# Ten blocks' own half block as a dense round outside the lists, in a two-layer graph attention kernel

## The chip, the cores and the metric

The kernel runs on one core of one Trainium2 chip. The metric is the device time of a run in microseconds (us), lower is better. The profile is of one execution; its span runs from the first to the last instruction.

## The reference

`x` has 3327 nodes of 512 features, `adj` is 3327 x 3327, sparse, with entries between 0.05 and 1 and a full diagonal. Edges crowd at low node numbers: the chance of an edge falls with the index of both nodes.

```
h = relu(layernorm(x))
x = x + (adj @ (relu(adj @ (h @ W1) + b1) @ W2) + b2)          # layer 0
h = relu(layernorm(x))
type_sum = adj @ h
attn_a = sigmoid(concat[type_sum, h] @ Wa.T + ba)              # attn_b alike
hs = h @ W_sa
scores = (hs @ a_left)[:, None] + (hs @ a_right)[None, :]
e = where(adj != 0, exp(-leaky_relu(scores, 0.01)), 0)
x_a = (e / (sum(e, 1) + 1e-5)) @ hs
x_b = adj @ (h @ W_gcnb) + b_gcnb
x = x + sigmoid(attn_a * x_a + attn_b * x_b)                   # layer 1
```

In layer 1, for each node, two weighted sums over its neighbours' rows of h are needed: one with the weights adj, one with the weights e. Multiplying the sums by the matrices W_gcnb and W_sa afterwards gives x_b and x_a.

## The kernel before, in words

The nodes are padded to 3328 and cut into NB = 26 blocks of 128. The host passes adj transposed, so a row of `adjT` is a source node j and a column a target node i.

*Layer 0* goes twice over all of adjT, in seven chunks of 512 columns (tiles of 128 x 512, or several tiles to a load). In the first pass the matmuls at L512 accumulate `acc_u`; at L516 DVE takes for each tile the largest magnitude in every group of GW = 32 columns (`most`). When a chunk is through, `make_lists` (L382) turns `most` into lists: for each block i and each of its two groups of columns q, in each half of 64 columns h, the numbers of the rows j that have a nonzero entry there. It is a generator that runs a step at a time beside the next chunk: flags, a scan, small matmuls `p_list` (L457), comparisons with `place_col`, sums. The number of a half's places is 64 times the block's number of *rounds*, `rooms[i]`, set by `list_rooms` for the given graph: 9, 8, 7, 6, 6 for blocks 1 to 5, five for 6 to 10, four for 11 to 18, three for the rest, 114 in all. If a list ran over, `overflow` would be set, and a dense branch at the end would do layer 1 anew. Block 0 is dense and is treated by itself ("hub").

For each round and group q, `gather_adj` issues one indirect load on POOL (L139, in `gather`) of 128 pieces of 32 columns of adjT into the tile `ae`. A gather is held behind a matmul of the passes by `pace`. The second pass (`acc_g`, L685) makes layer 0's output, its layernorm and the rows h of layer 1, stores the rows (520 wide, with the right score in column 512) in `h_dram`, and takes for each block the two logits of its own row (`own_logits`, two DVE products, L570).

*Layer 1* is a loop over i = 24 down to 2 (from L945), in which several blocks are in work at a time; the order of the work is written out by hand with `queued`, which puts instructions behind others in issue order. An iteration holds: `attend(i)`, which for each round and q issues an indirect load of 128 rows of h on POOL (L139, tiles `hr` and `rows`, 16 pairs of buffers), adds the scores on DVE (L800), takes the maximum (L804), the masked exponential (L206, ACT L207, L208) and the sum over the sources (L809); `weigh` of the block before the last, p_b (L883) and p_a (L890) on PE; `turn` of the last block, transposes `ptt` (L843) and copies to `tyT` on DVE (L858); the sums of exponentials on PE (L866); `sums(i)`, the neighbour sums `acc` (L829), eight matmuls of 64 x 64 by 512 columns to a round; `finish` of the block weighed (L739 to L764: DVE and ACT, a load of x1 on the SP queue and a store of the output on it); `copy_out` (ACT, L902 and L906). The first gather of attend(i) is paced behind the sums of an earlier block (LEAD = 3, or 4 for the blocks with high numbers). A block with more than SEG = 4 rounds does attend and sums in segments. After the loop block 1 and what is still open are finished.

Of the kernel before, what the change touches and what calls it, by code (L numbers as in the profile page):

```python
# [9 lines left out]
F32 = mybir.dt.float32  # L10
# [8 lines left out]
P = 128  # L19
# [15 lines left out]
LEAST_LOGIT = -88.0  # L35


def list_rooms(n_blocks):

    rooms = [0, 9, 8, 7, 6, 6] + 5 * [5] + 8 * [4]
    return (rooms + n_blocks * [3])[:n_blocks]


# [1 line left out]
def kernel(  # L47
# [23 lines left out]
    NCH = len(chunks)  # L71
    NG = NP // GW
    rooms = list_rooms(NB)
    first = [2 * sum(rooms[:i]) for i in range(NB)]
    NL = 2 * sum(rooms)

# [39 lines left out]
    overflow = kept([P, 1], "overflow", I32)  # L116


    ae = [kept([P, 2 * r, 2 * GW], f"ae{i}") if r else None for i, r in enumerate(rooms)]

    def segments(i):
        n = -(-rooms[i] // SEG)
        cuts = [-(-rooms[i] * k // n) for k in range(n + 1)]
        return list(zip(cuts, cuts[1:]))
    hubp = ctx.enter_context(tc.tile_pool(name="hubp", bufs=6))
    a_hub = hubp.tile([P, NB, P], F32, tag="a_hub", name="a_hub", bufs=1)
# [21 lines left out]
    def gather_adj():  # L148

        for i in range(1, NB):  # L150
            r = rooms[i]
            for k0, k1 in segments(i):
                for q in range(2):
                    for k in range(k0, k1):
                        while (i, q) not in listed:
                            yield None
                        f = first[i] + q * r + k
                        yield gather(
                            ae[i][:, 2 * k0 + q * (k1 - k0) + k - k0, :GW], adj_groups,
                            row_a[:, f : f + 1], NP * NG - 1,  # L160
                        )

    columns = gather_adj()

# [51 lines left out]
    with (  # L216
# [95 lines left out]
        MG = CW // GW  # L312
        NT = NB + 1
        begin = kept0([P, MG, NB], "begin", BF16)
        before = kept0([P, P], "before", BF16)
        shift = kept0([P, P], "shift", BF16)
        every = kept0([P, P], "every", BF16)
        steps = [kept0([P, MG, NT], f"step{k}", BF16) for k in range(2)]
        limit = kept0([P, NG], "limit", F32)
        size = kept0([P, NG], "size", F32)  # L320
        lower = kept0([P, 1], "lower", F32)
        place_row = kept0([P, max(rooms) * HALF], "place_row", F16)
        place_col = kept0([P, NL], "place_col", F32)
        group_col = kept0([P, NL], "group_col", F16)

        def make_constants():

            nc.vector.memset(begin, 1.0)
            nc.vector.memset(begin[:, :, 0:1], 0.0)
            for t in steps:  # L330
                nc.vector.memset(t[:, :, NB:NT], 1.0)
                nc.vector.memset(t[0:1, :, NB:NT], 0.0)
            yield
            nc.vector.memset(every, 1.0)

            for t, op, base in ((before, ALU.is_gt, 0), (shift, ALU.is_equal, -1)):
                nc.vector.memset(t, 1.0)
                nc.gpsimd.affine_select(
                    t, t, pattern=[[1, P]], compare_op=op, fill=0.0, base=base,
                    channel_multiplier=-1,  # L340
                )
            yield

            nc.vector.memset(lower, 1.0)
            nc.gpsimd.affine_select(
                lower, lower, pattern=[[0, 1]], compare_op=ALU.is_ge, fill=0.0, base=-HALF,
                channel_multiplier=1,
            )
            first_iota = nc.gpsimd.iota(
                place_row, pattern=[[1, max(rooms) * HALF]], base=0, channel_multiplier=0,  # L350
                allow_small_or_imprecise_dtypes=True,
            )
            tc.add_manual_dep(
                first_iota.ins, scaled[6].ins.name,
                mybir.DependencyInfo(mybir.DependencyClass.Sync, mybir.DependencyReason.DATA),
                reason="not among the first tiles",
            )
            behind = queued(first_iota)
            nc.gpsimd.memset(limit[:, :NQ], float(2 * NP))
            for r in sorted(set(rooms[1:])):  # L360
                i0, n = rooms.index(r), rooms.count(r)
                cols = slice(first[i0], first[i0] + n * 2 * r)
                nc.gpsimd.memset(limit[:, NQ * i0 : NQ * (i0 + n)], float(r * HALF))
                nc.gpsimd.iota(
                    place_col[:, cols], pattern=[[0, 2 * n], [HALF, r]], base=0,
                    channel_multiplier=1, allow_small_or_imprecise_dtypes=True,
                )
                nc.gpsimd.iota(
                    group_col[:, cols], pattern=[[NQ, n], [1, 2], [0, r]], base=NQ * i0,
                    channel_multiplier=0, allow_small_or_imprecise_dtypes=True,  # L370
                )
            yield
            for t, by in ((place_col, -float(HALF)), (group_col, 2.0)):
                nc.vector.scalar_tensor_tensor(
                    t, lower.to_broadcast([P, NL]), by, t, op0=ALU.mult, op1=ALU.add
                )
            yield
            for t in ae[1:]:
                nc.gpsimd.memset(t[:, :, :GW], 0.0)
            behind.close()  # L380

        def make_lists(c, most):  # L382
# [7 lines left out]

            flag = small([P, MG, NB], "flag", BF16)
            nc.vector.tensor_scalar(flag[:, :n, :], most[:, :n, :], 0.0, None, op0=ALU.is_gt)

            upto = small([P, MG, NB], "upto", BF16)
            flat = "p b j -> p (b j)"
# [97 lines left out]
        for c in range(NCH):  # L493
# [37 lines left out]
            with tc.issue_after(chunk_end.ins):  # L531
                if c == 1:
                    load_weights()
                if 0 < c <= HUB_LOADS:
                    load_hub(c - 1)
            lists = make_lists(c, most)
            next(lists)

# [25 lines left out]
                junk, h, 1.0, w_rows[:, s, :], op0=ALU.mult, op1=ALU.mult, accum_out=into  # L564
            )

        def own_logits(i, junk):

            for s in range(2):
                nc.vector.scalar_tensor_tensor(  # L570
                    junk, hrow[i % NR][:, :D], 1.0, w_own[:, s, :], op0=ALU.mult, op1=ALU.mult,
                    accum_out=node[i][:, 1 + s : 2 + s],
                )
            nc.vector.tensor_tensor(node[i][:, 1:3], node[i][:, 1:3], bab_row, ALU.add)
# [4 lines left out]
        def make_h1(c, sT):  # L579
# [49 lines left out]
            for i in blocks:  # L629
                store_next()  # L630

                if c < NCH - 2:
                    own_logits(i, l0w.tile([P, D], BF16, tag="junk", name=f"junk_{i}", bufs=1))
                yield

        rows_made = set()
# [130 lines left out]
    with tc.tile_pool(name="spw", bufs=2) as spw:  # L767
# [8 lines left out]
        def attend(i, seg):  # L776
# [10 lines left out]
            e = both[:, :, GW:]  # L787
            hr = taken[i][k0] = []
            for k in range(n):
                hr.append(next(pairs))  # L790
                for q in range(2):
                    f = first[i] + q * r + k0 + k
                    with queued(gathered[0]):
                        gathered[0] = gather(
                            hr[k][:, q, :], h_dram[:, :], row_h[:, f : f + 1], NP - 1
                        )
                    lead = LEAD[i < NB - 8]
                    if k0 + k + q == 0 and len(combined) >= lead:
                        pace(gathered[0], combined[-lead])
                nc.vector.tensor_tensor(  # L800
                    e.rearrange("p (q k) i -> p k q i", q=2)[:, k],
                    s_l, hr[k][:, :, D : D + 1].to_broadcast([P, 2, GW]), ALU.add,
                )
# [7 lines left out]
            )  # L811
            if k0:
                last = nc.vector.tensor_tensor(es, es, part, ALU.add)
            return last, exp

        def sums(i, seg):

            k0, k1 = seg  # L820
            n = k1 - k0
            if k0 == 0:
                taken[i]["acc"] = [bank(psA, f"acc_{i}_{h}") for h in range(2)]
            both = ae[i][:, 2 * k0 : 2 * k1, :]
            for k in range(n):
                for q in range(2):
                    for h in range(2):
                        half_p = slice(h * HALF, (h + 1) * HALF)
                        added = nc.tensor.matmul(  # L829
                            taken[i]["acc"][h][q * HALF : (q + 1) * HALF, :],  # L830
                            both[half_p, q * n + k, :], taken[i][k0][k][half_p, q, :D],
                            start=(k0 + k == 0), stop=(k1 == rooms[i] and k == n - 1),
                        )
            return added

# [83 lines left out]
        def some_logits(k, inst):  # L919
            n = len(late_rows)  # L920
            with queued(inst):
                for i in late_rows[n * k // 3 : n * (k + 1) // 3]:
                    own_logits(i, a_hub[:, :KD, :].rearrange("p k i -> p (k i)"))

        some_logits(0, made[0])
        for seg in segments(NB - 1):
# [190 lines left out]
```

## Time and profile before

| What | Value |
|---|---|
| Median of three runs | 836.6 us (833.45, 836.6, 841.8) |
| Profiled execution: span | 840.2 us (its time is told as this span) |
| Granted TensorE clock, mean of the span | 0.973 |
| Matrix engine (PE) matmul busy | 781.6 us, 3615 instructions |
| DVE busy | 515.6 us, 1658 instructions |
| ACT busy | 187.6 us, 396 instructions |
| POOL busy | 493.4 us, 513 instructions |
| Gathers from adjT / of rows of h | 228 / 140 + 88 |
| DMA traffic | 200.14 MB |
| Layer 1's loop, i = 24 to 2 | 471.2 to 798.3 us |

In a row of groups, "L829 PE MATMUL acc<-hr,ae" means line 829, the engine, the operation, the tile that is written and those that are read; then the count, the busy time, the mean duration in ns, and the time for which the engine stood still just before, with what ended most of it. "issue" there is waiting for nothing that the profile shows. In a table of stretches the columns are the stretch, its length, the busy times (and counts) of PE, of PE's weight loads, of DVE, ACT and POOL, the granted clock, the DMA share and GB/s.

### The profile page before, as it was taken

What the parts mean: (1) busy time and instruction counts of PE and PEld (TensorE: products, weight loads), DVE (VectorE), ACT (ScalarE), POOL (GpSimd) and SP (SyncE); (2) the same over time, 40 slices, a digit from 0 to 9 for tenths busy, and PEclk for the clock granted to TensorE, in tenths of its full rate; (3) what the DMA queues carried; (4) which work ended last, traced back from release to release, by engine and by line L of the source; (5) the groups of instructions that cost most, each with busy time, mean ns of one, the idle gap of its engine ahead of it and who ended that gap; (6) DMA issues with size and microseconds to landing.
All of it is one profiled execution on the core that took longest, in us unless ns stands there. A gap on an engine that the chain in (4) does not pass through costs nothing.

```text
span 840.2 us, 12143 instructions
## 1 busy us (share of the span) xinstructions
PE 781.6 (93%) x3615; PEld 416.9 (50%) x3615; DVE 515.6 (61%) x1658; ACT 187.6 (22%) x396; POOL 493.4 (59%) x513
## 2 busy tenths in 40 slices
PE   9999899999799999999999599799998999999795
PEld 7774344445443444444464366455554555454363
DVE  7778989999646866685775455345535353443342
ACT  7770000000002313033052022122222222121121
POOL 3202756676677777776716555666766767667400
PEclk9999999999799999999999799899999999999798
DMA  8787998898578989998958556787788867777600
GB/s 272 242 292 227 330 283 262 285 299 276 151 236 297 368 281 306 319 343 284 345 180 260 158 182 196 216 227 217 225 225 215 228 203 227 207 210 209 187 26 30
DMA packets 106891, 200.14 MB, mean 238 GB/s; under 512 B 16801, under 2 KB 30656, under 8 KB 106816
## 3 DMA queue, kind: packets, MB, share of 16 engines
q1 hardware_dynamic: 72592, 124.40, 45.2%
q0 software_dynamic: 25536, 63.74, 27.9%
q10 hardware_dynamic: 8688, 11.15, 3.8%
q8 instruction: 30, 0.49, 0.2%
q14 instruction: 45, 0.37, 0.1%
HBM read 179.39 MB, written 20.55 MB: 238 GB/s over the span
## 4 chain that ended last, share of the span: by engine, by line
PE 66%; issue 18%; DMA 7%; DVE 5%; another core or an unknown queue 3%; ACT 1%; SPq 0%; ACTq 0%; DVEq 0%
PE acc L829 14%; PE p_b L883 12%; PE p_a L890 11%; PE acc_g L685 10%; PE acc_u L512 5%; PE acc_hub L644 3%; DMA a<-in_adjT_dram 3%; PE ptt L843 3%; PE pu L291 3%; PE px L587 2%; DMA W_sa_sb<-in_W_sa_dram 1%; PE pt L283 1%; DMA xb<-in_x_dram 1%; DVE junk L563 1%
## 5 line engine op out<-in xcount | busy, mean ns | idle before, releaser
L139 POOL DMA_INDIRECT ae<-in_adjT_dram,row_a x228 | 246.4, 1081 | 151.6 <-issue 57.8
L139 POOL DMA_INDIRECT hr<-h_rows,row_h x140 | 144.1, 1029 | 64.5 <-issue 30.8
L685 PE MATMUL acc_g<-a,g 128*128 128x512 f32 (+1 forms) x364 | 160.3, 575 | 5.7 <-DMA a<-in_adjT_dram 3.8
L512 PE MATMUL acc_u<-a,rows 128*128 128x512 f32 (+1 forms) x364 | 159.9, 578 | 2.8 <-DMA a<-in_adjT_dram 2.2
L139 POOL DMA_INDIRECT rows<-h_rows,row_h x88 | 90.7, 1031 | 69.2 <-DVE e_hub L206 20.3
L883 PE MATMUL p_b<-W_g_sb,tyT 128*128 128x257 f32 x416 | 102.0, 395 | 16.3 <-issue 15.7
L516 DVE TENSOR_REDUCE most<-a 128x16 f32<-128x512 f32 (+1 forms) x182 | 110.6, 638 | 6.1 <-DMA a<-in_adjT_dram 5.2
L685 PEld LDWEIGHTS acc_g<-a,g 128*128 128x128 f32 x364 | 67.0, 192 | 85.5 <-issue 61.1
L883 PEld LDWEIGHTS p_b<-W_g_sb,tyT 128*128 128x128 f32 x416 | 78.3, 193 | 48.5 <-issue 19.3
L890 PE MATMUL p_a<-W_sa_sb,tyT 128*128 128x512 f32 (+2 forms) x216 | 97.5, 590 | 3.5 <-issue 3.1
L512 PEld LDWEIGHTS acc_u<-a,rows 128*128 128x128 f32 x364 | 66.5, 194 | 58.7 <-issue 51.9
L829 PE MATMUL acc<-hr,ae 64*64 64x512 f32 x560 | 81.7, 612 | 3.2 <-issue 2.3
L858 DVE COPY tyT<-ptt 128x512 f32<-128x512 f32 x51 | 34.9, 686 | 54.2 <-PE acc L829 21.8
L890 PEld LDWEIGHTS p_a<-W_sa_sb,tyT 128*128 128x128 f32 x216 | 41.1, 193 | 47.1 <-issue 45.6
L208 DVE SCALAR_TENSOR_TENSOR ae<-ae 128x192 f32<-128x192 f32 (+2 forms) x36 | 12.5, 368 | 79.1 <-issue 29.9
L829 PE MATMUL acc<-rows,ae 64*64 64x512 f32 x352 | 49.0, 607 | 1.7 <-issue 1.4
L829 PEld LDWEIGHTS acc<-hr,ae 64*64 64x64 f32 x560 | 30.9, 137 | 39.2 <-issue 37.9
L748 ACT ACTIVATE f<-f 128x2 f32<-128x2 f32 x26 | 5.3, 203 | 166.9 <-DVE f L747 118.4
L300 ACT ACTIVATE gT<-acc_u,b_col 128x512 f32<-128x512 f32 (+1 forms) x7 | 4.6, 657 | 157.1 <-issue 101.3
L563 DVE SCALAR_TENSOR_TENSOR junk<-rows,w_rows 128x512 bf16<-128x512 f32 x52 | 35.7, 686 | 3.0 <-issue 0.5
L716 DVE TENSOR_TENSOR xb<-xb,b_row 128x512 f32<-128x512 f32 x26 | 17.7, 689 | 30.4 <-DMA xb<-in_x_dram 19.6
L843 PEld LDWEIGHTS ptt<-ident,ty 128*128 128x128 f32 x208 | 24.5, 144 | 19.1 <-issue 18.2
(142 smaller groups left out, 907.5 us busy)
## 6 DMA issues: line engine op xcount, KB each, us to landing
a<-in_adjT_dram SPq DMA_DIRECT2D x338, 256.0 KB
h_rows<-rows SPq DMA_DIRECT2D x26, 260.0 KB
x<-in_x_dram SPq DMA_DIRECT2D x26, 256.0 KB
xb<-in_x_dram SPq DMA_DIRECT2D x26, 256.0 KB
x<-xb ACTq DMA_DIRECT2D x26, 256.0 KB
x1b<-x SPq DMA_DIRECT2D x26, 256.0 KB
out_dram<-va SPq DMA_DIRECT2D x25, 256.0 KB
ae<-in_adjT_dram,row_a POOLq DMA_INDIRECT x228
```

Source lines behind the costliest of these rows:

```text
L139: return nc.gpsimd.indirect_dma_start(out=dst, out_offset=None, in_=table, in_offset=bass.IndirectOffsetOnAxis(ap=rows, axis=0), bounds_ch ...
L291: nc.tensor.matmul(pu[:, :HID], hT[:, k, :], W1_sb[:, k, :], start=(k == 0), stop=(k == KD - 1))
L512: added = nc.tensor.matmul(acc[:, :w], u[j], a[:, :w], start=(j == 0), stop=(j == NB - 1))
L516: nc.vector.tensor_reduce(most[:, : w // GW, j], a[:, :w].rearrange("p (b i) -> p b i", i=GW), axis=AX.X, op=ALU.max, apply_absolute_value ...
L563: return nc.vector.scalar_tensor_tensor(junk, h, 1.0, w_rows[:, s, :], op0=ALU.mult, op1=ALU.mult, accum_out=into)
L644: nc.tensor.matmul(acc_hub[k], s, hrow[i % NR][:, :D], start=(i == 0), stop=(i == NB - 1))
L685: added = nc.tensor.matmul(acc[:, :w], g[j], a[:, j % per, :], start=(j == 0), stop=(j == NB - 1))
L829: added = nc.tensor.matmul(taken[i]["acc"][h][q * HALF : (q + 1) * HALF, :], both[half_p, q * n + k, :], taken[i][k0][k][half_p, q, :D], s ...
L843: moved = nc.tensor.transpose(pt[:, k * P : (k + 1) * P], ty[h][:, k * P : (k + 1) * P], ident)
L858: last = nc.vector.tensor_copy(dst, src)
L883: nc.tensor.matmul(p_b[n][:, :WH], tyT[:, k, 0, :], W_g_sb[:, k, n * WH : (n + 1) * WH], start=(k == 0), stop=(k == KD - 1),)
L890: last = nc.tensor.matmul(p_a[:, c0:c1], tyT[:, k, 1, :], W_sa_sb[:, k, c0:c1], start=(k == 0), stop=(k == KD - 1),)
```

## The change

For the ten blocks in `OWN` (1, 6, 7, 8, 12, 13, 14, 15, 17, 18) the sources in a target's own half block of 64 nodes leave the lists. They make one round of their own, round 0, with row j of half h in the place j: it needs no list, since its rows are consecutive.

- The entries of adjT for that round come by `load_own`: two plain loads on ACT's queue for each block (64 rows x 2 x 32 columns each), at the ends of chunks in the first pass.
- The rows of h for it come by one plain load on SP's queue into `h_own` (128 rows, three buffers), which serves both groups q, instead of two gathers.
- In `make_lists` the flags of the chunk's OWN blocks are multiplied by `apart`, which is 0 where a row lies in the group's own half block.
- `own_logits` of these ten blocks moves from the second pass into `attend`, where it reads `h_own`.
- `list_rooms` becomes 8, 7, 6, 5, 5 for blocks 1 to 5, four for 6 to 11, three for the rest: 97 list rounds, and with the ten dense ones 107 rounds. There are 194 gathers of each kind.
- `place_col` and `limit` are kept in 16-bit floats, `size` in bfloat16.

```diff
+OWN = 1, 6, 7, 8, 12, 13, 14, 15, 17, 18
-    rooms = [0, 9, 8, 7, 6, 6] + 5 * [5] + 8 * [4]
+    rooms = [0, 8, 7, 6, 5, 5] + 6 * [4]
     return (rooms + n_blocks * [3])[:n_blocks]
...
+    extra = [int(i in OWN) for i in range(NB)]
...
-                    for k in range(k0, k1):
+                    for k in range(max(k0, extra[i]), k1):
...
+    def load_own(i):
+
+        n = segments(i)[0][1]
+        for h in range(2):
+            rows = slice(i * P + h * HALF, i * P + (h + 1) * HALF)
+            nc.scalar.dma_start(
+                ae[i][h * HALF : (h + 1) * HALF, 0 : n + 1 : n, :GW],
+                adjT[rows, rows].rearrange("j (q i) -> j q i", i=GW),
+            )
...
+            own = [i - c0 // P for i in range(c0 // P, (c0 + w) // P) if extra[i]]
+            if own:
+                b0, b1 = own[0], own[-1] + 1
+                own = flag[:, b0 * NQ : b1 * NQ, c0 // P + b0 : c0 // P + b1]
+                nc.vector.tensor_tensor(
+                    own, own, apart[:, b0 * NQ : b1 * NQ, b0:b1], ALU.mult
+                )
...
                     load_hub(c - 1)
+                    for i in OWN:
+                        if c0 <= i * P + CW < c0 + CW:
+                            load_own(i)
...
-                if c < NCH - 2:
-                    own_logits(i, l0w.tile([P, D], BF16, tag="junk", name=f"junk_{i}", bufs=1))
+                if c < NCH - 2 and not extra[i]:
+                    own_logits(
+                        i, hrow[i % NR],
+                        l0w.tile([P, D], BF16, tag="junk", name=f"junk_{i}", bufs=1),
+                    )
...
-                hr.append(next(pairs))
-                for q in range(2):
-                    f = first[i] + q * r + k0 + k
+                if k0 + k < extra[i]:
+                    h = spw.tile([P, ROW], F32, tag="h_own", name=f"h_own_{i}", bufs=3)
+                    nc.sync.dma_start(h, h_dram[i * P : (i + 1) * P, :])
+                    hr.append(h.unsqueeze(1).to_broadcast([P, 2, ROW]))
+                    lists = ()
+                else:
+                    hr.append(next(pairs))
+                    lists = range(2)
+                for q in lists:
+                    f = first[i] + q * r + k0 + k - extra[i]
...
-                    if k0 + k + q == 0 and len(combined) >= lead:
+                    if k0 + k + q == extra[i] and len(combined) >= lead:
                         pace(gathered[0], combined[-lead])
...
             if k0:
                 last = nc.vector.tensor_tensor(es, es, part, ALU.add)
+            elif extra[i]:
+                own_logits(i, hr[0][:, 0, :], spw.tile([P, D], BF16, tag="junk", name=f"junk_{i}"))
```

In the built program the first three loads of `h_own` (18, 17, 15) stand on SP's queue ahead of the loop's first store of the output; each later one stands ahead of a store that is one iteration or more before its use (14 before the store of 20, 13 before that of 19, 12 of 17, 8 of 16, 7 of 15, 6 of 14, 1 of 10).

More of the change, by code (lines that the diff above doesn't have):

```diff
@@ L116 @@
     overflow = kept([P, 1], "overflow", I32)
-    ae = [kept([P, 2 * r, 2 * GW], f"ae{i}") if r else None for i, r in enumerate(rooms)]
+    ae = [
+        kept([P, 2 * (r + extra[i]), 2 * GW], f"ae{i}") if r else None for i, r in enumerate(rooms)
+    ]
     def segments(i):
-        n = -(-rooms[i] // SEG)
-        cuts = [-(-rooms[i] * k // n) for k in range(n + 1)]
+        r = rooms[i] + extra[i]
+        n = -(-r // SEG)
+        cuts = [-(-r * k // n) for k in range(n + 1)]
         return list(zip(cuts, cuts[1:]))
@@ L153, in gather_adj @@
                 for q in range(2):
-                    for k in range(k0, k1):
+                    for k in range(max(k0, extra[i]), k1):
                         while (i, q) not in listed:
                             yield None
-                        f = first[i] + q * r + k
+                        f = first[i] + q * r + k - extra[i]
                         yield gather(
@@ L314 @@
         begin = kept0([P, MG, NB], "begin", BF16)
+        apart = kept0([P, MG, CW // P], "apart", BF16)
         before = kept0([P, P], "before", BF16)
@@ L318 @@
         steps = [kept0([P, MG, NT], f"step{k}", BF16) for k in range(2)]
-        limit = kept0([P, NG], "limit", F32)
-        size = kept0([P, NG], "size", F32)
+        limit = kept0([P, NG], "limit", F16)
+        size = kept0([P, NG], "size", BF16)
         lower = kept0([P, 1], "lower", F32)
         place_row = kept0([P, max(rooms) * HALF], "place_row", F16)
-        place_col = kept0([P, NL], "place_col", F32)
+        place_col = kept0([P, NL], "place_col", F16)
         group_col = kept0([P, NL], "group_col", F16)
@@ L329, in make_constants @@
             nc.vector.memset(begin[:, :, 0:1], 0.0)
+            nc.vector.memset(apart, 1.0)
+            for b in range(CW // P):
+                for h in range(2):
+                    groups = slice(NQ * b + 2 * h, NQ * b + 2 * h + 2)
+                    nc.vector.memset(
+                        apart[h * HALF : (h + 1) * HALF, groups, b : b + 1], 0.0
+                    )
             for t in steps:
@@ L565, in score, with own_logits @@
             )
-        def own_logits(i, junk):
+        def own_logits(i, h, junk):
             for s in range(2):
                 nc.vector.scalar_tensor_tensor(
-                    junk, hrow[i % NR][:, :D], 1.0, w_own[:, s, :], op0=ALU.mult, op1=ALU.mult,
+                    junk, h[:, :D], 1.0, w_own[:, s, :], op0=ALU.mult, op1=ALU.mult,
                     accum_out=node[i][:, 1 + s : 2 + s],
@@ L630, in make_h1 @@
                 store_next()
-                if c < NCH - 2:
-                    own_logits(i, l0w.tile([P, D], BF16, tag="junk", name=f"junk_{i}", bufs=1))
+                if c < NCH - 2 and not extra[i]:
+                    own_logits(
+                        i, hrow[i % NR],
+                        l0w.tile([P, D], BF16, tag="junk", name=f"junk_{i}", bufs=1),
+                    )
                 yield
@@ L831, in sums @@
                             both[half_p, q * n + k, :], taken[i][k0][k][half_p, q, :D],
-                            start=(k0 + k == 0), stop=(k1 == rooms[i] and k == n - 1),
+                            start=(k0 + k == 0), stop=(k1 == rooms[i] + extra[i] and k == n - 1),
                         )
@@ L922, in some_logits @@
                 for i in late_rows[n * k // 3 : n * (k + 1) // 3]:
-                    own_logits(i, a_hub[:, :KD, :].rearrange("p k i -> p (k i)"))
+                    own_logits(i, hrow[i % NR], a_hub[:, :KD, :].rearrange("p k i -> p (k i)"))
         some_logits(0, made[0])
```

## The prediction

> **What bounds the kernel now.** I read the page's busy shares first, then the slices, the chain, the rows of the gathers, and last the busy times by stage.
>
> ```profile
> span 840.2 us, 12143 instructions
> PE 781.6 (93%) x3615; PEld 416.9 (50%) x3615; DVE 515.6 (61%) x1658; ACT 187.6 (22%) x396; POOL 493.4 (59%) x513
> ...
> PE   9999899999799999999999599799998999999795
> POOL 3202756676677777776716555666766767667400
> ...
> PE 66%; issue 18%; DMA 7%; DVE 5%; another core or an unknown queue 3%; ACT 1%; SPq 0%; ACTq 0%; DVEq 0%
> ...
> L139 POOL DMA_INDIRECT ae<-in_adjT_dram,row_a x228 | 246.4, 1081 | 151.6 <-issue 57.8
> L139 POOL DMA_INDIRECT hr<-h_rows,row_h x140 | 144.1, 1029 | 64.5 <-issue 30.8
> ...
> L139 POOL DMA_INDIRECT rows<-h_rows,row_h x88 | 90.7, 1031 | 69.2 <-DVE e_hub L206 20.3
> ```
>
> PE carries the chain, but 18% of it is "issue": PE stood still with no wait that the profile shows. To see where, I cut the attention loop into its iterations i = 24 to 2, 471.2 to 798.3 us, by the first p_b matmul of each. Columns: stretch, its length, then PE, PEld, DVE, ACT and POOL busy.
>
> ```profile
> 484.70:527.90 43.20, 43.20 (x244) 26.61 (x240) 21.73 (x76) 10.95 (x24) 26.97 (x26) 1.00 0.65 201
> 527.90:546.50 18.60, 14.16 (x64) 7.46 (x60) 6.16 (x25) 2.89 (x7) 12.63 (x13) 0.82 0.75 209
> 546.50:607.40 60.90, 59.57 (x343) 35.27 (x340) 30.85 (x103) 15.05 (x31) 42.61 (x42) 1.00 0.79 224
> 607.40:676.50 69.10, 65.07 (x360) 35.85 (x358) 31.00 (x112) 14.43 (x32) 47.89 (x48) 1.00 0.79 219
> ```
>
> The first stretch is iterations 23 to 20 (three rounds each): 10.80 us each, PE never idle. The chain's pieces for an iteration give 3.67 (p_b) + 3.43 (p_a) + 0.87 (ptt) + about 0.2, and 2.63 for the 24 small matmuls of three rounds. So **nominal = 8.2 + 0.87 x rounds**: 11.7 for four, 12.55 for five, 15.2 for eight. Rounds of blocks 24 to 2 are 114 - 3 - 9 = 102, so 23 x 8.2 + 102 x 0.87 = 277.3 us, against 327.1 measured: **49.8 us are lost to stalls**. By iteration: 24: 2.7; 23–20: 0; 19: 7.8; 18–14: 2.5; 13–9: 9.0; 8–6: 6.5; 5–4: 6.6; 3: 4.2; 2: 10.6.
>
> What goes with them? The list of line 829's tile, first for iterations 23–20, then for 607.4 to 754:
>
> ```profile
>   issue: 3.1, 16
> ```
> ```profile
>   issue: 31.5, 90
>   remote: 16.4, 7
> ...
>   DVE tyT L858: 19.4, 7
> ```
>
> In the late stretch acc matmuls sit idle for no shown reason, and DVE's tyT copies start 19.4 us "waiting for acc" long done. PE's progress shows late on the other engines. It happens while POOL issues gathers without a pause (one each 1.30 us: 1.0 busy and 0.3 issue), and stops when POOL stops. With six gathers to an iteration (7.8 us of POOL in 10.8) nothing is lost; with eight (10.4 in 11.7) 0.5 us each; with ten (13.0 in 12.55, POOL never rests) 2 to 3 us; 19 follows upon the step from six to eight. The data are not late: gathers are issued three or four blocks ahead. I infer the link from this coincidence; no view names it.
>
> **The Trainium skill.** "Perfetto Trace Analysis", DMA Instruction — SWDGE (GPSIMD), says that the reported end of a GpSimd DMA is the end of descriptor generation, not of the data. The trace agrees: 1.03 us busy, but 3 to 5 us from issue to landing. "DMA: Bandwidth & Descriptors", SWDGE vs HWDGE vs iDMA, says that GpSimd computes descriptors in software and appends them to rings, while loads from SP and ACT do not use that path. So ten plain loads lift work off POOL; a link from that path to PE's stalls is in neither page. "TensorE: Matmul & The Clock Gate", Part 1, has the array at half rate after an idle window: the trace gives a granted clock of 0.82 in the stretch 527.9–546.5, so a stall costs something after it too.
>
> **The change, part by part.**
> 1. *Rounds.* Lists fall from 114 to 97; ten blocks get a dense round: 107. Blocks 2, 3, 4, 5, 9, 10 and 16 lose one round each, and 1 and the other OWN blocks none. 7 x 0.87 = **-6.1 us** of PE, on the path.
> 2. *Gathers.* 2 x 97 = 194 of each kind instead of 228: 34 less x 1.30 = 44 us of POOL for h rows in the loop. Blocks 12–25 now issue six, 6–11 eight, 5 and 4 ten, 3 twelve, 2 fourteen, 1 sixteen. POOL need over nominal PE time: 0.67 for 18–12 (block 16, with three rounds, 0.72), 0.9 at most for 11–6, 1.04 for 5 and 4, 1.16 for 3, 1.27 for 2. Stalls left, taken from what the same ratio lost before: 24 unchanged 2.7; 19 3.0 (four fewer gathers after it, 5 of its 7.8 us); 18–14 0.3; 13–9 1.6; 8–6 2.6 (gathers of the big blocks, three ahead, fall here); 5–4 4.3; 3 2.1; 2 2.7. Sum 19.3 instead of 49.8: **-30.5 us**. If the link is not there: 0. If every stall goes: -49.8.
> 3. *h_own loads.* Ten of 260 KB on SP. By the skill's fit in "DMA: Bandwidth & Descriptors", Anatomy of one DMA, 2.0 + bytes/436e3 gives an estimate of 2.6 us each; the gathers of that size took 3 to 5, which I use. The issue order puts three ahead of the first store and the others one to three iterations before use, so 12 us of cover stand over 5. They can hold stores of out behind them on SP by a few us (nobody waits for these). Price 0; without cover 5 us for each block. Bytes fall: 34 gathers of 260 KB less, ten loads more, 6.4 MB of 200.
> 4. *load_own.* 20 small strided loads on the ACT queue at the ends of chunks in the first pass, where 34 small gathers vanish. ACT is nearly empty there (2.06 of 80 us between 120 and 200). Price 0; at worst 20 x 0.1 us of issue.
> 5. *Lists.* 68 p_list matmuls and weight loads less (3 us of PE), one batch less and narrower DVE work (about 4 us), five products with `apart` more (0.8). In 120–200 PE is busy 77.8 and DVE 76.7 of 80: either bounds. I take **-3** (0 to -4).
> 6. *own_logits.* Two 688 ns products and a small sum move for ten blocks from the second pass (PE and DMA bound, so no gain) into the attention, 1.5 us of DVE per block. There DVE is busy 31 of 60.9 us. Behind it stand tyT copies and the finish; hidden by DVE's spare half. Price 0; uncovered 15 us in all.
> 7. *Tail* (798.3 to 840.2): block 1 keeps nine rounds, no gathers: 0.
>
> Sum -6.1 - 30.5 - 3 = -39.6: span 800.6. The median stands to this span as 836.6 to 840.2 (0.9957), so **797 us**.
>
> **The rivals.**
> - *A: the late stalls stay.* The stall belongs to sums with big lists or to POOL runs of eight already. Only 19 to 12 get better, say -12. For it: blocks 11–1 still issue eight or more, and stalls grow down the list. Against: eight per iteration lost only 0.5 us each in 18–14. -6.1 - 12 - 3 = -21: span 819, 816 us.
> - *B: PE only.* POOL has nothing to do with it: -6.1 - 3: span 831, 827.5 us. For it: the profile calls the idle time "issue". Against: iterations 23–20, same instructions, none lost.
> - *C: slower.* The dense round comes late: h_own stands on SP behind a store that itself waits for the finish, attend's first DVE add waits for it, and tyT copies queue behind that add. Each block late by L costs 10 L; from L = 4 us the gain is gone. At 5 us: 800.6 + 50 = 851, 847 us. For it: SP is in order, and h_own has only three buffers. Against: a buffer is reused three OWN blocks later, freed by sums at least an iteration before, and the issue order has the load ahead.
> - *The change doesn't do what it says*: lists with fewer places overflow and the fallback branch runs, hundreds of us. With these inputs the fullest list just fits, so I give this next to nothing.
>
> **How the numbers follow.** The likeliest, 0.62; its own range 780 (all stalls gone: 840.2 - 6.1 - 49.8 - 3 = 781, 778 us) to 807 (half of the gain in stalls is missing). A 0.22 (807 to 822), B 0.08, C and small mishaps that eat all 0.08. The range 780 to 820 leaves out B, C and the edges. One per cent is about what can be told from no change: faster 0.92, same 0.04, slower 0.04.
>
> **What would show it.** Right: POOL at some 415 us busy, 194 gathers of each kind; PE's "issue" share of the chain well under 18%; iterations 18 to 6 within 0.5 us of nominal and iteration 19 near 14 us; acc's wait "remote" and tyT's wait for acc nearly gone; the first pass 3 us shorter. Wrong: iterations of eight gathers still at 14 to 15 us (A); stalls as before though POOL rests (B); DVE or PE waiting for h_own, or tyT late behind own_logits (C).

## The result and the profile after

The kernel after takes 796.9 us (median of four runs, 796.48 to 797.28), the kernel before 836.6 us beside it: ratio 0.951, 95% interval 0.946 to 0.956. The profiled execution's span is 795.6 us against 840.2.

First the page of the kernel after, with the lines that answer to those shown of before (lines of code move: L139 is now L145, L829 is L875).

```profile
span 795.6 us, 11711 instructions
PE 755.1 (95%) x3491; PEld 412.4 (52%) x3491; DVE 507.7 (64%) x1650; ACT 185.4 (23%) x394; POOL 416.6 (52%) x442
...
PE   9999999999889899999999789989999999999995
POOL 2301666776666867774000664566566676676500
...
PE 40%; DVE 2%; issue 1%; DMA 1%; another core or an unknown queue 1%; POOL 0%; ACT 0%; DVEq 0%; POOLq 0%
...
L145 POOL DMA_INDIRECT ae<-in_adjT_dram,row_a x194 | 206.1, 1063 | 134.7 <-issue 55.9
...
L145 POOL DMA_INDIRECT hr<-h_rows,row_h x120 | 123.3, 1028 | 67.3 <-PE acc L875 28.4
L145 POOL DMA_INDIRECT rows<-h_rows,row_h x74 | 75.4, 1019 | 114.5 <-ACT e_hub L223 72.9
```

POOL lost 77 us of work and PE 26.5, and what POOL waits for longest ahead of the loads into `hr` is now PE's sums (28.4 us), no longer "issue": it has pauses. The chain's shares cannot be set beside those of before as they stand: they add up to 45%, because this chain reaches back only to 437 us. Asked for the attention loop alone, the chain of before and then of after:

```profile
by line: PE acc L829 33.5%; PE p_b L883 27.3%; PE p_a L890 25.6%; issue 8.4%; PE ptt L843 6.7%; PE p_b L866 1.3%; PE p_b L871 0.0%
```

```profile
by line: PE acc L875 31.8%; PE p_b L929 30.7%; PE p_a L936 28.1%; PE ptt L889 7.0%; issue 1.2%; PE p_b L912 1.2%; PE p_b L917 0.0%
```

So "issue" in the loop's chain fell from 8.4% of 327.1 us to 1.2% of 287.1 us.

The same cut into iterations, for the loop's stretches in after: 23–20, 19, 18–14, 13–9, 8–2. Columns as before: stretch, length, busy PE, PEld, DVE, ACT, POOL, then granted clock.

```profile
481.20:524.50 43.30, 43.30 (x245) 26.63 (x241) 21.77 (x76) 10.98 (x24) 26.62 (x26) 1.00 0.66 201
524.50:540.10 15.60, 13.25 (x63) 7.23 (x61) 6.26 (x25) 2.86 (x6) 10.02 (x10) 0.89 0.78 214
540.10:597.60 57.50, 57.50 (x335) 35.16 (x333) 34.31 (x120) 13.94 (x30) 33.19 (x32) 1.00 0.69 209
597.60:656.10 58.50, 58.50 (x343) 35.60 (x341) 33.06 (x112) 14.00 (x30) 40.28 (x40) 1.00 0.78 237
656.10:754.70 98.60, 97.48 (x558) 54.59 (x556) 53.17 (x207) 22.21 (x50) 63.77 (x63) 1.00 0.71 213
```

PE is busy without a gap in three of the five stretches; 18–14 and 13–9 took 60.9 and 69.1 us before. The whole loop, before and then after:

```profile
471.20:798.30 327.10, 308.82 (x1643) 172.16 (x1643) 151.69 (x541) 67.61 (x146) 215.73 (x210) 0.97 0.73 209
467.60:754.70 287.10, 283.62 (x1586) 167.67 (x1586) 158.76 (x572) 64.78 (x143) 179.86 (x176) 0.98 0.71 211
```

PE's idle time in the loop fell by only 14.8 us (18.3 to 3.5), its busy time by 25.2, of which seven rounds explain about 6. So more than half of what the stalls cost was counted as "busy": the longest matmul of `acc` is recorded with 1110 ns in before and 641 in after, at a median of 589 in both. It is the length of an iteration, not PE's busy share, that shows the stalls in full. Last the list of the acc tile over the whole loop, before and then after:

```profile
  issue: 54.5, 173
  remote: 41.7, 11
...
  DMA hr<-h_rows,row_h: 0.6, 1
...
  DMA rows<-h_rows,row_h: 0.3, 1
...
  DVE tyT L858: 21.8, 8
```

```profile
  issue: 36.5, 147
...
  remote: 1.4, 2
...
  DVE tyT L904: 6.1, 3
```

The waits "for another core or an unknown queue" ("remote") and tyT's late starts, by which the stalls were known, are nearly gone. Waits for the gathered rows themselves were 0.9 us in before's list, which speaks against late data as the cause. In time: the loop began at 471.2 and begins at 467.6 (-3.6), took 327.1 and takes 287.1 us (-40.0), and the tail fell from 41.9 to 40.9.

### The profile page after: what moved, and what is told of

Its sections match the earlier page's. It is cut to its first block, busy times and chain, and to the rows that moved or that the text cites. A ratio compares the mean times of both kernels' runs of the same rounds, so it can differ in the third digit from the quotient of the medians.

```text
span 795.6 us, 11711 instructions
## 1 busy us (share of the span) xinstructions
PE 755.1 (95%) x3491; PEld 412.4 (52%) x3491; DVE 507.7 (64%) x1650; ACT 185.4 (23%) x394; POOL 416.6 (52%) x442
## 5 line engine op out<-in xcount | busy, mean ns | idle before, releaser
L145 POOL DMA_INDIRECT ae<-in_adjT_dram,row_a x194 | 206.1, 1063 | 134.7 <-issue 55.9
L722 PE MATMUL acc_g<-a,g 128*128 128x512 f32 (+1 forms) x364 | 157.9, 570 | 5.9 <-DMA a<-in_adjT_dram 4.7
L145 POOL DMA_INDIRECT hr<-h_rows,row_h x120 | 123.3, 1028 | 67.3 <-PE acc L875 28.4
L145 POOL DMA_INDIRECT rows<-h_rows,row_h x74 | 75.4, 1019 | 114.5 <-ACT e_hub L223 72.9
L936 PE MATMUL p_a<-W_sa_sb,tyT 128*128 128x512 f32 (+2 forms) x216 | 95.2, 585 | 0.3 <-issue 0.3
L875 PE MATMUL acc<-hr,ae 64*64 64x512 f32 x480 | 63.4, 602 | 0.7 <-issue 0.4
L875 PE MATMUL acc<-rows,ae 64*64 64x512 f32 x296 | 38.8, 618 | 4.7 <-issue 4.6
L875 PEld LDWEIGHTS acc<-hr,ae 64*64 64x64 f32 x480 | 26.3, 134 | 25.7 <-issue 25.2
L624 DVE TENSOR_TENSOR xb<-px,xb 128x512 f32<-128x512 f32 x26 | 17.0, 683 | 26.2 <-issue 12.8
```

Of the source, the lines that this page charges most:

```text
L145: return nc.gpsimd.indirect_dma_start(out=dst, out_offset=None, in_=table, in_offset=bass.IndirectOffsetOnAxis(ap=rows, axis=0), bounds_ch ...
L624: nc.vector.tensor_tensor(x1, px, x1, ALU.add)
L722: added = nc.tensor.matmul(acc[:, :w], g[j], a[:, j % per, :], start=(j == 0), stop=(j == NB - 1))
L875: added = nc.tensor.matmul(taken[i]["acc"][h][q * HALF : (q + 1) * HALF, :], both[half_p, q * n + k, :], taken[i][k0][k][half_p, q, :D], s ...
L936: last = nc.tensor.matmul(p_a[:, c0:c1], tyT[:, k, 1, :], W_sa_sb[:, k, c0:c1], start=(k == 0), stop=(k == KD - 1),)
```

## The experiments

All ratios are to the kernel before, run beside the experiment on the same chip. One fact has to come first, since I had not reckoned with it: **the kernel before took 837 us on two of the five chips of these experiments and 763 to 764 us on the other three**. No chip was met twice, so "a chip with stalls" below can also mean a chip in a passing condition. "Lost" is a loop's time over 8.2 + 0.867 x rounds for each iteration: 277.0 us for the kernel before (102 of its 114 rounds lie in the loop) and 271.0 for after (95 of 107).

**1. Half the gathers, on a chip where before takes 764 us.** Edit to the kernel before:

```diff
-                hr.append(next(pairs))
-                for q in range(2):
+                pair = next(pairs)
+                hr.append(pair[:, 0, :].unsqueeze(1).to_broadcast([P, 2, ROW]))
+                for q in range(1):
```

> The kernel before, with one indirect load of rows of h to a round instead of two (114 instead of 228): the rows of the first group of columns serve both groups, so the second group's neighbour sums are of wrong rows. Rounds, matmuls and DVE work stay as they were. Theory (PE stalls go with POOL's unbroken runs of gathers): the loop i = 24 to 2 falls from 327 us to its nominal 277 plus 2 to 5, time about 790 us. Rival (PE only: the lost time belongs to PE and its small matmuls): 832 to 840 us, the late iterations still at 14 to 18 us.

Measured: 760.1 us, ratio 0.9946 (0.9926 to 0.9965). The loop took 277.0 us, nothing lost; but the kernel before, only 4 us slower here, cannot have lost 50. Both expectations missed: there was next to nothing to remove.

**2. A plain load in place of the second gather, same chip.**

```diff
                 hr.append(next(pairs))
-                for q in range(2):
+                nc.sync.dma_start(hr[k][:, 1, :], h_dram[i * P : (i + 1) * P, :])
+                for q in range(1):
```

> As the run with half the gathers, but the other half of each buffer pair is filled by a plain load of 260 KB on SP's queue (the block's own rows, so the second group's sums are of wrong rows). The bytes are again those of before, POOL's instructions are not. Theory: 790 to 797 us, as with half the gathers. Rival (the gathers' traffic on the DMA engines stalls PE): 825 to 840 us.

Measured: 759.4 us, 0.994 (0.992 to 0.9961), loop 277.0. Not decisive for the same reason.

**3. POOL filled with memsets in place of the second gather, same chip.**

```diff
                 hr.append(next(pairs))
-                for q in range(2):
+                for _ in range(2):
+                    nc.gpsimd.memset(hr[k][:, 1, :], 0.0)
+                for q in range(1):
```

> As the run with half the gathers, but POOL fills the other half of each buffer pair with zeros in two memsets of 128 x 520, some 1.3 us together, as long as a gather and its issue (the second group's sums are thus zero). POOL is then as full as before, with half the descriptors. If what counts is descriptor generation: 790 to 797 us. If what counts is that POOL is busy without a pause: 825 to 840 us.

Measured: 763.4 us, 0.9994 (0.9976 to 1.0012); nothing lost after the loop's first iteration. Not decisive.

**4. The dense round's rows gathered again, same chip.** Edit to the kernel after (`row_own` holds i x 128 + p in column i):

```diff
-                if k0 + k < extra[i]:
-                    h = spw.tile([P, ROW], F32, tag="h_own", name=f"h_own_{i}", bufs=3)
-                    nc.sync.dma_start(h, h_dram[i * P : (i + 1) * P, :])
...
+                    at = row_h[:, f : f + 1] if k0 + k >= extra[i] else row_own[:, i : i + 1]
+                        gathered[0] = gather(hr[k][:, q, :], h_dram[:, :], at, NP - 1)
```

> The kernel after, with the dense round's rows of h fetched by two indirect loads with consecutive row numbers into a buffer pair, instead of one plain load on SP. Rounds stay at 107, the gathers of h go back from 194 to 214. Theory: stalls return in iterations 19 to 12 and 8 to 6, where the ten blocks' gathers fall: 812 to 820 us. Rival (PE only): 795 to 800 us, since the rounds are those of after.

Measured: 753.0 us, 0.9854 (0.9815 to 0.9893). The loop took 271.0 us with 214 gathers: nothing lost. This chip pays for rounds only. It gives a clean price of the rounds, though: 277.0 us in runs 1 and 2, 271.0 here, for seven rounds less: 0.86 us each.

**5. The kernels before and after, on another chip.**

> The kernel before, unchanged, for a profile on the chip of these runs. The four runs ahead of it came with 764 us for this kernel instead of 836.6, and their attention loops had no stall in any iteration. If the stalls belong to the chip (or its condition) and not to the kernel: a span near 764 with every iteration at 8.2 + 0.87 x rounds on such a chip, a span near 838 with 50 us of stalls on one like the first. If they belong to the kernel, 50 us of stalls anywhere.

Measured: span 838.8 us (a single run; 27 others of this kernel on the chip have a median of 837.1), 50.2 us lost, spread over the iterations as in the first profile (19: 6.2; 18–14: 3.8; 13–9: 9.8; 8–2: 27.5).

> The kernel after, unchanged, beside the kernel before on the chip of these runs. On a chip without stalls only the rounds and the lists are left of the prediction's sum: 6.1 + 3 = 9.1 us, ratio 0.988 (0.985 to 0.992). On one with stalls: 0.951 as before.

Measured: 793.9 us beside 837.1, ratio 0.9472 (0.9447 to 0.9497); 15.1 us lost. The first result repeats. The same kernel before takes 837 us here and 764 on the chip of runs 1 to 4; it was not profiled there, but none of the four kernels that were had stalls after the loop's first iteration.

**6. own_logits back in the second pass, same chip as 5.** Edit to the kernel after:

```diff
-                if c < NCH - 2 and not extra[i]:
+                if c < NCH - 2:
...
-            elif extra[i]:
-                own_logits(i, hr[0][:, 0, :], spw.tile([P, D], BF16, tag="junk", name=f"junk_{i}"))
```

> The kernel after, with own_logits of the ten blocks taken in the second pass again. The prediction gave the move a price of 0: within 1 us of the kernel after. If the move into attend cost what DVE has to do more in the loop: up to 15 us faster than after; if the second pass had room for it only at a price, up to 7 us slower.

Measured: 795.1 us, 0.9496 (0.9463 to 0.953), against 0.9472 (0.9447 to 0.9497): the medians are 1.3 us apart and the intervals overlap, so no price can be told. A gain of 15 us is excluded; a price of 0 fits.

**7. LEAD 3, 3 in the kernel before, same chip as 5.**

```diff
-LEAD = 3, 4
+LEAD = 3, 3
```

> The kernel before with LEAD 3, 3 instead of 3, 4: from block 17 on gathers stay paced three blocks ahead of the sums, so there is no double run of gathers in iteration 19. Rounds and gathers are unchanged. On a chip with stalls, if they go with the length of a run of gathers: iteration 19 falls from 18.6 to 11 to 13 us, 5 to 8 us in all. If they go with the number of gathers alone: within 1.5 us. On a chip without stalls: within 1.5 us.

Measured: 839.2 us, 1.0028 (1.0009 to 1.0048). Of the table of stretches, iteration 19, then 12 to 9 and 8 to 6 (with the lines that answer in the kernel before on this chip below it: 19, 18–14, 13–9, 8–6 and, for run 9, 5–2):

```profile
527.90:538.70 10.80, 10.80 (x62) 6.65 (x60) 5.80 (x23) 2.74 (x6) 7.18 (x8) 1.00 0.79 230
610.00:671.90 61.90, 55.67 (x290) 31.14 (x288) 27.11 (x97) 13.04 (x29) 41.62 (x41) 0.97 0.78 218
671.90:722.70 50.80, 46.74 (x230) 24.96 (x229) 20.48 (x79) 8.84 (x21) 34.42 (x34) 0.95 0.75 208
```

```profile
526.30:543.30 17.00, 13.28 (x62) 6.58 (x60) 4.97 (x17) 2.65 (x5) 11.35 (x12) 0.90 0.74 214
543.30:605.50 62.20, 60.12 (x345) 35.23 (x341) 31.67 (x111) 15.17 (x32) 43.53 (x43) 1.00 0.78 223
605.50:675.40 69.90, 65.03 (x359) 35.34 (x357) 30.96 (x113) 14.52 (x33) 48.40 (x48) 0.98 0.78 218
675.40:719.00 43.60, 42.32 (x230) 23.22 (x228) 19.26 (x74) 9.28 (x21) 30.73 (x30) 1.00 0.75 217
719.00:796.70 77.70, 69.06 (x362) 34.23 (x360) 32.18 (x118) 14.21 (x30) 48.96 (x49) 0.96 0.72 204
```

The double run of gathers is gone from iteration 19, and its stall with it, all 6.2 us: rounds and gathers are unchanged, only their bunching. So where a stall falls goes with the bunching. How much is lost in all does not show it: 13–6 lost 27.0 us instead of 15.8, the whole loop 51.8 instead of 50.2. That the time came back because of the shorter lead is a guess; no run tests it. Half of the expectation is met (iteration 19), and the gain of 5 to 8 us in all is missed: the sum is near what "the number of gathers alone" would give, 2.1 us from before.

**8. Repeats of 2 and 4, on a third chip.**

> The kernel before with one of each round's two indirect loads replaced by a plain load of 260 KB on SP's queue (the block's own rows, so the second group's sums are of wrong rows), again, since the first time it ran on a chip without stalls. Rounds and bytes are those of before, the gathers of h are 114 instead of 228. On a chip with stalls (kernel before near 837 us): if the stalls go with POOL's runs of gathers, the loop's excess over 8.2 + 0.87 x rounds falls from 48 to under 6 us: 785 to 797 us. If they go with the traffic of the DMA engines or with PE's own work: 825 to 840 us. On a chip without stalls: 0.994 of before, as then.

> The kernel after with the dense round's rows fetched by two indirect loads on POOL instead of a plain load on SP, again on another chip: 214 gathers of h instead of 194, rounds as after. On a chip with stalls: if they go with the runs of gathers, the excess of iterations 18 to 9 goes from 0 back to 5 to 10 us, and that of 8 to 6 from 2 to 5 or more: 806 to 820 us. If only the rounds count: 793 to 800 us, as after. On a chip without stalls: 0.985 of before, as then.

Measured: 759.5 us, 0.9948 (0.9927 to 0.9968), and 755.1 us, 0.9872 (0.982 to 0.9924), with before at 763.9: again a chip without stalls, loops of 277.0 and 271.0 us. They repeat 2 and 4 and decide nothing more. One reading of them matters, iterations 19, 18–14, 13–9 and 8–6 of the kernel after with its rows gathered:

```profile
496.90:507.70 10.80, 10.80 (x64) 6.65 (x60) 5.59 (x20) 2.75 (x6) 8.45 (x8) 1.00 0.79 247
507.70:565.20 57.50, 57.50 (x336) 35.14 (x332) 35.21 (x124) 14.02 (x31) 44.66 (x42) 1.00 0.80 241
565.20:623.60 58.40, 58.40 (x345) 35.63 (x341) 33.02 (x111) 13.91 (x30) 45.06 (x44) 1.00 0.84 246
623.60:661.20 37.60, 37.60 (x231) 22.80 (x229) 25.03 (x98) 9.62 (x23) 29.16 (x28) 1.00 0.80 241
```

POOL is as full here (45 of 58 us) as where the kernel before stalls (48 of 70), and PE has no gap. With the 0.3 us of issue to each gather, 44 gathers fill 58.3 of the 58.4 us of 13–9: POOL issues indirect loads without any pause. So neither a crowded POOL nor an unbroken run of gathers is enough to stall PE; it takes a chip with stalls besides.

**9. Two substitutes for the second gather in one kernel, by block.** Edit to the kernel before:

```diff
                 hr.append(next(pairs))
-                for q in range(2):
+                if 11 <= i <= 18:
+                    for _ in range(2):
+                        nc.gpsimd.memset(hr[k][:, 1, :], 0.0)
+                elif i <= 10:
+                    nc.sync.dma_start(hr[k][:, 1, :], h_dram[i * P : (i + 1) * P, :])
+                for q in range(1 if i <= 18 else 2):
```

> The kernel before with one of each round's two indirect loads replaced in two ways: for blocks 18 to 11 by two memsets on POOL of 1.3 us together (the second group's half is zero), for blocks 10 to 1 by a plain load of 260 KB on SP (the second group's rows are wrong). Rounds stay at 114. On a chip with stalls, where before loses 6 to 8 us in iteration 19 and 37 us in 13 to 2: if the stalls go with indirect loads in an unbroken run, iteration 19 takes 10.8 to 13 us and 13 to 2 lose under 6 us, about 790 us in all. If POOL's being busy is enough, iteration 19 stays at 17 to 19 us. If traffic or PE's own work makes them, 13 to 2 still lose 30 us or more. On a chip without stalls: 0.995 of before, nothing lost.

Measured: 791.2 us beside 837.1, 0.9444 (0.9369 to 0.952): a chip with stalls, and 114 rounds. Iterations 19, 18–14, 13–9, 8–6, 5–2:

```profile
526.20:537.00 10.80, 10.80 (x62) 6.65 (x60) 5.42 (x20) 2.86 (x6) 9.10 (x14) 1.00 0.67 193
537.00:595.40 58.40, 58.40 (x344) 35.64 (x341) 32.35 (x103) 14.57 (x31) 42.38 (x59) 1.00 0.47 147
595.40:655.40 60.00, 60.00 (x358) 36.53 (x356) 32.57 (x116) 14.73 (x34) 24.55 (x23) 1.00 0.76 235
655.40:693.00 37.60, 37.60 (x232) 22.79 (x228) 20.17 (x79) 9.14 (x21) 16.14 (x16) 1.00 0.80 258
693.00:749.20 56.20, 56.20 (x365) 33.72 (x361) 30.23 (x108) 13.32 (x29) 24.01 (x23) 1.00 0.82 265
```

PE has no gap from iteration 23 on: 1.4 us lost in the whole loop instead of 50 (the kernel before was profiled on the chip of runs 5 to 7, not on this one; the lines to compare stand in run 7). In the last three stretches rounds, matmuls and the bytes for each round are those of before, and the DMA engines move more per us than there (235 to 265 GB/s against 204 to 218); only half of the indirect loads are gone. So neither PE's own work nor traffic makes the stalls. In iteration 19 POOL is busy 9.1 of 10.8 us and in 18–14 42.4 of 58.4, with memsets for half of its gathers; before it was 11.4 of 17.0 and 43.5 of 62.2, with 6.2 and 3.8 us lost. So POOL's being busy doesn't make them either. What counts is the indirect loads, on a chip that is touched by them. Whether it is their number in a stretch or their following one another without a pause, this run doesn't tell: it halves both.

**10. Three dense rounds gathered again, and a ramp of the lead.** Edits to the kernel after: blocks 8, 7 and 6 gather their dense round's rows as in 4, and

```diff
+RAMP = {
+    17: ("sums", 20, 3), 16: ("turn", 20, -1), 15: ("p_a", 20, 3),
+    14: ("p_a", 19, 1), 13: ("p_b", 18, 7), 12: ("p_b", 17, 3),
+}
...
+                    if k0 + k + q == plain and i in RAMP:
+                        pace(gathered[0], marks[RAMP[i][:2]][RAMP[i][2]])
```

> The kernel after with two edits that fall in different iterations. One: the dense rounds of blocks 8, 7 and 6 fetch their rows by two indirect loads each again (ten gathers a block as before the change, five rounds as before and after). Two: the step from LEAD 3 to LEAD 4 at block 17 is stretched over blocks 17 to 12, each block's first gather paced behind a matmul one to three us earlier than the last, so that no two blocks' gathers run together. On a chip with stalls, if they go with unbroken runs of indirect loads: iteration 19 falls from 15.4 to 10.8 to 12 us, and iterations 12 to 9, with 0.1 us lost in after, lose 3 to 9 us again. If the ten blocks' plain loads gave nothing and only the fewer list rounds did: 12 to 9 stay within 0.5 us. On a chip without stalls: 0.985 to 0.99 of before and nothing lost anywhere.

Measured: 757.0 us beside 762.8, 0.9928 (0.9904 to 0.9952): a chip without stalls, loop 271.0 us. Neither edit could show anything.

## Why the prediction was right

The median came out at 796.9 where 797 was forecast. That is closer than the working deserves, and luck: the span fell by 44.6 us where the sum said 39.6. The profile of before, probably of its slowest run, lay 3.6 us above its median, that of after 1.3 us below its own, and the two errors cancel. On the second chip the medians fell by 43.3 us.

| Step | Forecast | Measured, first pair of profiles |
|---|---|---|
| Seven rounds | -6.1 | -6.0 (277.0 to 271.0 on chips without stalls) |
| Stalls left: 24 / 19 / 18–14 / 13–9 | 2.7 / 3.0 / 0.3 / 1.6 | 2.8 / 4.8 / 0.0 / 0.2 |
| Stalls left: 8–6 / 5–4 / 3 / 2 | 2.6 / 4.3 / 2.1 / 2.7 | 1.8 / 2.4 / 2.3 / 1.8 |
| Stalls left, sum | 19.3 of 49.8 | 16.1 of 50.0 |
| Ahead of the loop | -3 | -3.6 (-1.8 on the second chip) |
| Tail | 0 | -1.0 |

*A misreading at the start.* The prediction took the 18% of "issue" in the chain of the whole span for PE standing still. Most of it is not PE's: between 106 and 201 us, in the first pass, the chain runs over ACT's copies, and four gaps of ACT between them (16.4, 26.7, 25.2 and 25.2 us) are 93 of those 149 us, while PE is busy (77.8 of the 80 us from 120 to 200). In the loop the share is 8.4%, some 27 us. The second profile of before has the same stalls and 3% of "issue", since its chain takes another way. The sum doesn't rest on this share, only on the lengths of the iterations; but as a sign of being right, "well under 18%" meant little.

*Stalls (step 2).* The inference, stalls go with POOL's unbroken gathers, was the step on which 30 of 40 us hung, and it was only a coincidence in one trace. Run 9 confirms that the gathers make the stalls: with half of them replaced the stalls go, at equal rounds, and in 13 to 2 at equal bytes. The narrower part, that they must be unbroken, is not shown: run 7 moved a stall by moving a run of gathers, but lost as much in all. The rule "POOL's need over PE's" placed the remaining stalls fairly: next to nothing in 18 to 9, 7 and 6, where it is at most 0.9, and 0.9 to 2.3 us each in 5 to 2, where it is over 1. Iteration 8, at 0.83, lost 1.8 us against it. Iteration 19 was sized too low: twelve gathers in a row still cost 4.8 us.

What the step left out is the chip. "If the link is not there: 0" was priced for a wrong reading; it comes near to the case on three of five chips. In the kernels profiled there no iteration after the loop's first stalled; the kernel before was not among them, and being some 4 us slower than the half-gather kernels of runs 1 and 2, it may lose a little. There the change is left with rounds and whatever else it saves: 0.985 and 0.987 for after with its dense rows gathered. The kernel after itself was not run on such a chip.

*Rounds (step 1)* held to 0.1 us. *h_own and own_logits (steps 3 and 6)*: price 0; in the kernel after nothing is put down as waiting for the loads of h_own, and run 6 finds no price for the logits within the intervals.

*Lists (step 5)*: the size came out near, the reason did not. The first pass's last matmul starts at 220.0 before and at 219.2 after, where 3 us were forecast. On the three chips without stalls it starts at 210.2 to 212.8 us in the kernels with the old lists and at 210.9 to 212.8 in those with the new ones. So the shorter lists bought next to nothing. The loop begins 3.6 and 1.8 us earlier on chips with stalls; before's own starts there spread from 469.5 to 472.1, so even that is hardly clear. The 34 fewer gathers from adjT are a possible source, not shown.

*Rivals.* A (late stalls stay) fails: 8–2 lost 28.1 us and lose 8.3. B (PE only) fails here, where the stalls do go with the gathers; on chips without stalls only its small gain is left. C (slower) did not happen: iterations 18 to 12, where six of the ten h_own blocks fall, lost nothing.

*Open:* how the stall gain splits between the ten plain loads (20 gathers) and the fewer list rounds (14). The runs made for it (4, the second of 8, and 10) all met chips without stalls. Open too is whether spacing the same gathers out would help, what differs between the chips, or in their condition, and by what path a gather holds up PE.

## What to carry to other kernels

Where the busiest engine loses time that no wait explains, cut its work into equal iterations, fit time against work, and set the excess of each beside what the other engines do then. A share of the chain is no substitute: ask for the stretch, and see whose gaps they are. On a chip with stalls, closely spaced indirect loads on POOL held up PE though no wait named them: in run 9, with half of them replaced by plain loads on another queue or by memsets, the loss fell from 50 us to 1.4. Rows with consecutive numbers can come by such a plain load. And measure on more than one chip before a gain of this kind is taken for the kernel's: 5% on one kind was 1.3 to 1.5% on another, for a version with the same rounds.

## What the runs showed of the hardware that I had not expected

- The same kernel took 837 us on two chips and 763 to 764 us on three. Set against the half-gather kernels of runs 1 and 2 (759 to 760 us), the loop accounts for 50 us. The passes ahead of it account for some 30, for a cause that no run shows: the loop begins at 469.5 to 472.1 us with before's gathers from adjT on chips with stalls (run 9 too, at 470.7), and at 438.0 to 441.0 on those without. The change recovers little of these 30 us (3.6 and 1.8).
- A gather costs POOL the same on both kinds of chip: 1035 ns busy on average for a gather of h without stalls (run 4), 1031 with (before, in run 5). What differs is how far PE gets meanwhile.
- On a chip without stalls POOL issued indirect loads with no pause but the 0.3 us of issue through iterations 18 to 9, and PE had no gap (run 8).
- Without stalls the loop holds to 8.2 us + 0.867 us for each round to within 0.1 us over 23 iterations.
